# A smaller descriptor space for GpSimd, and two more feature buffers that are loaded early

## The chip, the core and the metric

The kernel runs on one core of a Trainium2 chip. A core has five engines with a queue of instructions each: TensorE (PE in the profile, with PEld for its weight loads), VectorE (DVE), ScalarE (ACT), GpSimd (POOL) and SyncE (SP), and 16 DMA engines that all queues share. The metric is the device time of one execution in microseconds (us). Three runs of the kernel before took 311.9, 312.74 and 313.98 us; the median is 312.74 us.

## What is computed

There are 16384 tokens of 256 features (`r_feat`) and a segment number from 0 to 7 for each (`r_bids`). Here is the reference, cut to what matters:

```python
q, k, v = feat @ Wq, feat @ Wk, feat @ Wv          # 32, 32 and 256 wide
starts = jnp.searchsorted(bids, jnp.arange(B, dtype=bids.dtype))
pos = jnp.arange(N, dtype=bids.dtype) - starts[bids]
# rows are put at [bids, pos] of a (8, 3072) frame; the mask says which places are filled
scores = jnp.einsum('bld,bmd->blm', qp, kp)
attn = softmax(jnp.where(mask[:, None, :], scores, NEG))
rp = jnp.einsum('blm,bmd->bld', attn, vp)
r = rp[bids, pos]
t = r @ Wt
tn = (t - t.mean(axis=0)) / jnp.sqrt(t.var(axis=0) + EPS) * gamma + beta
return feat + relu(tn)
```

The segment numbers are not sorted, so a segment's frame takes in only those of its tokens that lie within 3072 of its start. All other tokens read a row at an edge of a frame. So a few thousand tokens have a row of their own, and every other token gets its features plus one of a few rows that are the same for many tokens. The mean and the variance run over all tokens, so no output can be finished before the attention of all segments is done.

## The kernel before, in words

The program (`fast_path`, from line 900) is written as one list of operations. A small class records which bytes each operation reads and writes, and puts a semaphore wait where two operations on different queues touch the same bytes. Each engine runs its own operations in the order of the list, so the place of a line in the source is its place in its engine's queue.

**Stages.** First come the tables: which tokens belong to which segment, by matrix products and comparisons. Then a loop over the segments `e` = 0 to 7 (lines 1683 to 1830). Segment `e` has 4 to 6 tiles of 128 rows. Its rows are gathered from HBM by GpSimd (`gather`, line 882) into `xs`, two segments ahead; TensorE makes scores and attended rows; they end in `tk`, and SP stores them to `t_rows` in HBM. In the last loop (from line 1895), which I call the tail, the output is written, in two ways:

- *Groups.* The tokens are cut into 16 groups of 1024 tokens, 1 MB of features each. A group is loaded into a buffer `fb[i % NF]` (`group_in`, line 1670, on SP's queue), gets its shared row added, and is stored to `out` as a whole (line 1918). Two groups make a pair, and there are 8 passes `c`, one a pair. In each, TensorE makes the shared rows by a one-hot product (`hot`); VectorE adds half of the buffer, and for the other half TensorE adds the features by an identity product and ScalarE copies the sum back into the buffer. At the end of pass `c` VectorE normalises the own rows of segment `c` (`rows(c)`: two tensor-tensor operations and one more on `tk`).
- *Puts.* The own rows overwrite their places in `out`: GpSimd scatters each tile of 128 rows by an indirect DMA (`put`, line 892). There are 39 puts for the eight segments (their own groups must be stored before), and two for tokens that share a place (`tl`).

**What orders stores, loads and puts.** SP's queue is in order. After store `i` it waits for store `i-2` to land and then counts up the semaphore `done` (`finish`, line 1890); after that come the reloads that are listed for this store:

```python
1670    def group_in(i, after=()):
1671        pg.dma("SP", fb[i % NF][:], feat3[ORDER[i]], after)
1893    LATER = {5: (9, 10), 6: (11, 12), 7: (13,), 8: (14,), 9: (15,)}
1916            f = fb[i % NF]
1920            if i >= 2:
1921                finish(stores[i - 2])
1922                for k_ in LATER.get(i, ()):
1923                    group_in(k_)
```

GpSimd's puts of segment `e` wait until `done` has reached the number of the last group that holds a token of that segment's reach; after that wait the puts follow one another. At the very end GpSimd waits until all puts have landed.

**Memory.** There are 9 group buffers (`NF` = 9, line 956). They lie over the work space of the stages before (from `lm` to `sq`), so they can be loaded only when that part is no longer needed: groups 0 to 4 in the loop over `e` = 6 (lines 1725 to 1769), 5 and 6 in segment 7 (line 1797), 7 and 8 just before the tail (line 1834), and 9 to 15 in the tail by `LATER`. A small buffer `rsq` (line 979) holds squares of the repeated rows; `eb` (two buffers of 2 KB a partition) holds the token codes for the one-hot tables, and `sel`, `st_t` and `ss` lie over it for later use.

GpSimd's indirect DMAs take their descriptors from a space in SBUF that the compiler sets aside, 16 KB of each partition unless another size is given to `bacc.Bacc` (line 1996).

Of the kernel before, what the change touches and what calls it, by code (L numbers as in the profile page):

```python
# [9 lines left out]
F32 = mybir.dt.float32  # L10
# [9 lines left out]
P = 128  # L20
NB = 8
# [6 lines left out]
FT = 6  # L28
# [871 lines left out]
def fast_path(nc, feat, bids, wq, wk, wv, wt, gamma, beta, out, bad):  # L900
    N, D = feat.shape
# [4 lines left out]
    GT = 8  # L906
# [9 lines left out]
    end = start  # L916
    plan = []

    def at(name, shape, dtype, off):
        h = nc.alloc_sbuf_tensor_at(name, shape, dtype, offset=off)  # L920
        pg.place(h, "SB", off, mybir.dt.size(dtype))
        return h

    def new(name, shape, dtype=F32):
        nonlocal end
        size = mybir.dt.size(dtype)
        for d in shape[1:]:
            size *= d
        plan.append((name, shape, dtype, end))
        h = at(name, shape, dtype, end)  # L930
        end += size + -size % 32
        return h

    def addr(h):
        return pg.where[h.name][1]
# [5 lines left out]
    lm = new("lm", [P, NL, J + 3], BF16)  # L941
# [11 lines left out]
    vs[1] = new("vs1", [P, FT, D + 1])  # L953
    pb = new("pb", [P, FT, QB])
    sq = [new(f"sq{i}", [P, D]) for i in range(4)]
    NF = 9
    fb = [at(f"f{i}", [P, GT, D], F32, addr(lm) + 8192 * i) for i in range(NF)]
    assert end >= addr(lm) + 8192 * NF

    ident, ones, irow = new("ident", [P, P]), new("ones", [P, P]), new("irow", [P, P])  # L960
    ones_n = new("ones_n", [P, P])
# [3 lines left out]
    xl, tl = new("xl", [P, LT, D]), new("tl", [P, LT, D])  # L965
    eb = [new("eb0", [P, GT * P], BF16), new("eb1", [P, GT * P], BF16)]
    sel = at("sel", [P, FT, P], F32, addr(eb[0]))
    st_t = at("st_t", [P, 2 * D], F32, addr(eb[0]))
    ss = at("ss", [P, 2 * D], F32, addr(eb[1]))
    ye = at("ye", [P, D], F32, addr(acc) + 1024)  # L970
# [5 lines left out]
    cbeg, cend, n_bc = new("cbeg", [P, NL]), new("cend", [P, NL]), new("n_bc", [P, NL])  # L976
    n_1 = new("n_1", [P, NL])
    later = new("later", [P, 2])
    rsq, cnt7, e7, ew = new("rsq", [P, D]), new("cnt7", [P, 2]), new("e7", [P, 2]), new("ew", [P, 2, FT])
    mask, idx = new("mask", [P, TT]), new("idx", [P, TT + LT], I32)  # L980
    reads_r, rdens = new("reads_r", [P, TT]), new("rdens", [P, TT])
    jc, lr, pad = new("jc", [P, FT]), new("lr", [P, FT]), new("pad", [P, FT])
# [231 lines left out]
    def gather_reads(e, tiles, after):  # L1214
        for t in tiles:
            m = e * FT + t
            pg.gather(reads_r[:, m : m + 1], reads_of, idx[:, m : m + 1], N, after=[after])
# [262 lines left out]
    def slot(n=1):  # L1480
        for _ in range(n):
            if work:
                work.pop(0)()
# [155 lines left out]
    def one_hot():  # L1639
        C = NG // 2  # L1640

        def part(c):
            def go():
                x = eb[c % 2]
                pg.set("DVE", x[:], 99.0)
                for r in range(2):
                    pg.dma(
                        "SP", x[64 * r : 64 * r + 6 * NB, :],
                        edge_of[ORDER[2 * c + r] * GT * P : (ORDER[2 * c + r] + 1) * GT * P].unsqueeze(0).to_broadcast(
                            [6 * NB, GT * P]  # L1650
                        ),
                    )

            def end():
                pg.ts(hot[:, c, :, :], eb[c % 2][:].rearrange("e (p i) -> e i p", i=GT), emod[:], ALU.is_equal)

            return go, end

        ps = [part(c) for c in range(C)]
        todo = [ps[0][0]]  # L1660
        for c in range(C):
            if c + 1 < C:
                todo.append(ps[c + 1][0])
            todo.append(ps[c][1])
        return todo
# [4 lines left out]
    def group_in(i, after=()):  # L1670
        pg.dma("SP", fb[i % NF][:], feat3[ORDER[i]], after)

# [20 lines left out]
    for e in range(NB - 1):  # L1693
        n = e + 1
        for eng in ("PE", "ACT", "DVE"):
            pg.register(eng, n, tiles_i[0:1, n : n + 1], 2)
        if e == 1:
            todo, choose = tables()
            work.extend(todo)
        if e == 2:  # L1700
            work.extend(one_hot())
            work.append(choose)
        ahead = e + 2
        LTs = FT if ahead < NB else LT
        for u in range(FT):
            if ahead <= NB and u == 0 and e:
                first = list_half(ahead, 0, ps_s[2])
            attend(e, u)
            if e == 0 and u == 0:
                second_list()  # L1710
                attended(e, u)
                first = list_half(ahead, 0, ps_s[2])
            if ahead <= NB and u == 0:
                first()
                if LTs == FT:
                    second = list_half(ahead, 1, ps_s[3])
            slot(int(u in steps.get(e, range(FT))))
            if u == 4 and e + 3 <= NB and e:
                list_tests(e + 3, FT if e + 3 < NB else LT)
            if u == 4:  # L1720
                values(n, 0)
            if u == 5:
                values(n, 1)
            if e == NB - 2 and u == 3:
                group_in(1)
            if (e, u) != (0, 0):
                opened = attended(e, u)
            if u == 0:
                if ahead <= NB and LTs == FT:
                    second()  # L1730
                if ahead == NB:
                    others()
                xt_main(n, 0)
                xt_main(n, 1)
            if u == 1:
                xt_rest(n)
                project(n, 0)
                scores(e, 1, None)
            if u == 3:
                project(n, 1)  # L1740
                scores(n, 0, range(4))
            if u == 4:
                scores(n, 0, range(4, 6))
            if u == 5:
                values(n, 2)
            for x in ready:
                moments(*x)
            ready = []
            lag.append((e, u))
            for _ in range(0 if e == 0 else 2 if u % 2 else 1):  # L1750
                if lag:
                    square(*lag[0])
                    ready.append(lag.pop(0))
            if e == 0 and u == 1:
                pg.tr32(gb[:].rearrange("p s i -> p (s i)"), graw[:].rearrange("p s i -> p (s i)"))
                for e_ in range(3, NB):
                    pg.dma(
                        "SP", xs[:, e_ * FT : (e_ + 1) * FT, :], zt[:].unsqueeze(1).to_broadcast([P, FT, D]), [opened]
                    )
            if e == 0 and u in (1, 5):  # L1760
                pg.copy("ACT", spot[:], ones[:, 0:1])
            if (e, u) in reads_at:
                gather_reads(*reads_at[e, u], opened)
            if e == NB - 2 and u == 1:
                group_in(0)
            if e == NB - 2 and u > 3:
                group_in(u - 2)
            if e == NB - 2 and u == 5:
                group_in(4)
            if e == 4 and u == 3:  # L1770
                pg.set("POOL", tk[:, TT - 2 : TT, :], 0.0)
                pg.register("POOL", "writes", writes[:], 16 * (6 * NB + LT), 16 * (4 * NB + LT - 1))
                pg.register("POOL", "lastg", lastg[:], NG, 1)
                pg.register("POOL", "third", third_l[:], 1)
                for e_ in range(NB):
                    pg.register("POOL", ("g", e_), upto[0:1, e_ : e_ + 1], NG, 1)
                    pg.register("POOL", e_, tiles_i[0:1, e_ : e_ + 1], 2)
    slot(99)

    e = NB - 1  # L1780
# [13 lines left out]
    for u in range(4):  # L1794
        attend(e, u)
        if u == 3:
            group_in(5)
            group_in(6)
        if u == 0:
            pg.tt(weights, weights, ew[:, 0, :], ALU.add)  # L1800
        if u == 3:
            attended(e, u)
            choose_rows(0)
            choose_rows(1)
        for x in ready:
            moments(*x)
        ready = [(e, u)]
        if u == 1:
            for t in range(3, FT):
                m = e * FT + t  # L1810
                pg.ts(by_reads[:, t - 3, :], ones_n[:], reads_r[:, m : m + 1], ALU.mult)
        if u != 3:
            attended(e, u)
        if u == 2:
            scores(e, 1, None)
        if u < 3:
            repeated(u)
# [13 lines left out]
    pg.mm(sums[:], we[:], ecat[0 : 2 * NB, :, :].rearrange("p s d -> p (s d)"), start=False, stop=True)  # L1831
    choose_rows(3)
    pg.mm(b_e[:, 0:D], ident[:], ecat[:, 0, :], start=False, stop=True)
    for i in range(7, NF):
        group_in(i)
    for t in range(LT):
        pg.gather(tl[:, t, :], t_rows, ridl[:, t : t + 1], NB * FW)
# [1 line left out]
    def unit(i, x):  # L1839
        return fb[i % NF][:, x : x + 2, :].rearrange("p t d -> p (t d)")  # L1840

# [48 lines left out]
    def finish(w):  # L1890
        pg.op("SP", lambda e: e.sem_inc(done, 1), [], [], after=[w])  # L1891

    LATER = {5: (9, 10), 6: (11, 12), 7: (13,), 8: (14,), 9: (15,)}
    stores = []
    for c in range(NG // 2):
        pair = (2 * c, 2 * c + 1)
# [18 lines left out]
        for i in pair:  # L1915
            f = fb[i % NF]
            stores.append(
                pg.op("SP", lambda e, i=i, f=f: e.dma_start(out3[ORDER[i]], f[:]), [f[:]], [], dma=True)
            )
            if i >= 2:  # L1920
                finish(stores[i - 2])
                for k_ in LATER.get(i, ()):
                    group_in(k_)
# [86 lines left out]
```

## Time and profile before

| | |
|---|---|
| median of three runs | 312.74 us |
| the profiled execution | 313.58 us |
| its span, first to last instruction | 311.3 us |
| busy: PE, DVE, ACT, POOL | 254.0, 226.2, 138.7, 132.9 us |
| moved by DMA | 56.81 MB |
| group loads, group stores | 16 each, of 1024 KB |
| puts of segment rows, of repeated rows | 39 and 2 |
| mean granted TensorE clock | 0.918 |

Times in the profile are microseconds from the start of the span, unless a duration is given in ns (the mean of a group of instructions, or minimum, median and maximum). A row of the timeline has start, length, engine, line, operation, what is written and read, and in brackets how long the engine had been idle and what ended that. The engine's name with a q (SPq, POOLq) means its sequencer. "Landing" is the time from the issue of a DMA to its completion. The line of an instruction is often that of a helper, so the tile's name tells more. In a table of stretches the columns are busy time with the number of instructions for PE, PEld, DVE, ACT and POOL (or for POOL alone), then the granted clock, the busy share of the DMA engines, and GB/s.

### The profile page before, as it was taken

The page shows a single profiled execution, that of the slowest core. Times are in us where ns is not written, and L with a number is a line of the kernel's source. Part 1 is how long each engine was busy: PE and PEld are TensorE (multiplying, and loading weights), DVE is VectorE, ACT ScalarE, POOL GpSimd, SP SyncE. Part 2 cuts the span into 40 slices and gives each one's busy share as a digit, 9 for nine tenths or more (in the row PEclk, how much of TensorE's full clock was granted, in tenths as well). Part 3 has the DMA queues.
Part 4 walks back from the last instruction along what each step waited for, and adds up shares of the span by engine and source line. Part 5 has one row for each costly group of instructions (what it writes and reads, how often), then busy time and mean ns, then how long its engine had stood idle before and what let it go on. Part 6 is the DMA issues. An engine that isn't in the chain of part 4 may idle for free.

```text
span 311.3 us, 4501 instructions
## 1 busy us (share of the span) xinstructions
PE 254.0 (82%) x1204; PEld 168.3 (54%) x1204; DVE 226.2 (73%) x712; ACT 138.7 (45%) x298; POOL 132.9 (43%) x155
## 2 busy tenths in 40 slices
PE   1779688899798898999999999989969978673800
PEld 1655565766576677687868778757533322221200
DVE  7866778679999896737664774777389999992820
ACT  7346234267474728544754583564432222121110
POOL 3435580340250061006322754742230278887774
PEclk9989796999999999999999999999998977789565
DMA  3102069422122021112131321679997899999995
GB/s 98 35 24 60 11 194 346 161 87 69 52 75 78 28 75 30 67 57 80 32 95 36 90 90 28 196 244 379 359 394 312 365 346 420 425 419 418 418 411 193
DMA packets 23238, 56.81 MB, mean 183 GB/s; under 512 B 4768, under 2 KB 15858, under 8 KB 19114
## 3 DMA queue, kind: packets, MB, share of 16 engines
q1 hardware_dynamic: 17434, 45.77, 39.5%
q0 software_dynamic: 5232, 10.18, 10.1%
q10 hardware_dynamic: 544, 0.52, 0.5%
q8 instruction: 13, 0.21, 0.3%
q14 instruction: 15, 0.12, 0.1%
HBM read 26.73 MB, written 28.61 MB: 178 GB/s over the span
## 4 chain that ended last, share of the span: by engine, by line
PE 40%; DVE 31%; DMA 11%; issue 7%; ACT 6%; POOL 2%; SPq 1%; DVEq 0%; POOLq 0%; ACTq 0%
PE ps L807 38%; DMA out<-f 6%; DMA f<-in_r_feat 5%; DVE acc L846 4%; DVE tk L826 2%; DVE w L826 2%; DVE f L826 2%; DVE junk L833 2%; POOL out L892 2%; PE ps L812 2%; DVE k L823 2%; ACT pa L817 1%; DVE ge L835 1%; ACT xT L817 1%; ACT tk L817 1%
## 5 line engine op out<-in xcount | busy, mean ns | idle before, releaser
L882 POOL DMA_INDIRECT xs<-in_r_feat,idx x48 | 51.0, 1063 | 101.5 <-DVE idx L846 77.3
L807 PE MATMUL ps<-vs,pa 128*128 128x257 f32 x312 | 73.6, 384 | 4.7 <-ACT sq L817 3.6
L807 PEld LDWEIGHTS ps<-vs,pa 128*128 128x128 f32 x312 | 57.2, 190 | 16.5 <-ACT sq L817 4.8
L892 POOL DMA_INDIRECT out<-tk,idx x39 | 46.1, 1182 | 25.9 <-SPq L1891 14.6
L807 PE MATMUL ps<-f,ident 128*128 128x512 f32 x64 | 41.8, 778 | 12.8 <-DMA f<-in_r_feat 12.8
L817 ACT ACTIVATE tk<-ps,rdens 128x256 f32<-128x256 f32 x46 | 22.2, 482 | 61.8 <-DVE rdens L859 61.7
L822 ACT COPY f<-ps 128x512 f32<-128x512 f32 x32 | 17.1, 590 | 53.3 <-PE ps L807 53.3
L807 PE MATMUL ps<-wvt,xT 128*128 128x256 f32 x156 | 39.7, 406 | 0.3 <-ACT pa L817 0.3
L807 PEld LDWEIGHTS ps<-wvt,xT 128*128 128x128 f32 x156 | 31.1, 204 | 11.0 <-issue 4.3
L807 PEld LDWEIGHTS ps<-f,ident 128*128 128x128 f32 x64 | 13.3, 235 | 29.1 <-DMA f<-in_r_feat 17.1
L846 DVE SCALAR_TENSOR_TENSOR acc<-sq,reads_r,acc 128x256 f32<-128x256 f32 x45 | 21.6, 480 | 8.8 <-ACT sq L817 8.8
L817 ACT ACTIVATE pa<-ps,mask 128x512 f32<-128x512 f32 x39 | 24.0, 689 | 7.6 <-PE ps L807 7.4
L826 DVE TENSOR_TENSOR f<-f,ps 128x512 f32<-128x512 f32 x32 | 20.0, 682 | 7.7 <-DMA f<-in_r_feat 7.1
L826 DVE TENSOR_TENSOR tk<-tk,ss 128x1024 f32<-128x1024 f32 (+1 forms) x30 | 24.4, 850 | 0.3
L882 POOL DMA_INDIRECT reads_r<-reads_of,idx x12 | 13.4, 1119 | 24.8 <-ACT sq L817 11.9
L846 DVE SCALAR_TENSOR_TENSOR acc<-tk,reads_r,acc 128x256 f32<-128x256 f32 x45 | 21.5, 478 | 1.2 <-ACT tk L817 0.7
L807 PE MATMUL ps<-q,k 32*128 32x512 f32 (+2 forms) x154 | 21.1, 482 | 1.5 <-ACT pa L817 1.1
L807 PE MATMUL ps<-xT,w 128*128 128x512 f32 (+1 forms) x60 | 20.7, 478 | 0.6 <-ACT xT L817 0.5
L823 DVE COPY k<-ps 32x128 f32<-32x128 f32 x40 | 11.8, 294 | 12.2 <-PE ps L807 11.3
L807 PE MATMUL ps<-vs,pb 128*128 128x257 f32 x82 | 19.6, 387 | 0.0
L807 PEld LDWEIGHTS ps<-vs,pb 128*128 128x128 f32 x82 | 15.1, 189 | 6.5 <-issue 2.3
L817 ACT ACTIVATE q<-ps,cqk 96x512 f32<-96x512 f32 (+3 forms) x24 | 14.6, 607 | 7.7 <-PE ps L807 7.4
(258 smaller groups left out, 355.3 us busy)
## 6 DMA issues: line engine op xcount, KB each, us to landing
f<-in_r_feat SPq DMA_DIRECT2D x16, 1024.0 KB, 11.7
out<-f SPq DMA_DIRECT2D x16, 1024.0 KB, 10.3
t_rows<-tk SPq DMA_DIRECT2D x8, 512.0 KB, 4.8
xs<-zt SPq DMA_DIRECT2D x5, 768.0 KB, 10.5
t_rows<-tk SPq DMA_DIRECT2D x8, 256.0 KB, 2.3
eb<-edge_of SPq DMA_DIRECT2D x16, 96.0 KB, 2.3
xs<-in_r_feat,idx POOLq DMA_INDIRECT x48, 2.8
out<-tk,idx POOLq DMA_INDIRECT x39, 7.3
```

The lines of the kernel that those rows point to most:

```text
L807: "PE", lambda e: e.matmul(out, lhsT, rhs, start=start, stop=stop, skip_group_check=True),
L812: return self.op("PE", lambda e: e.transpose(out, in_, ident), [in_, ident], [out])
L817: "ACT", lambda e: e.activation(out, in_, func, bias=bias, scale=scale), [in_, *more], [out]
L822: return self.op("ACT", lambda e: e.copy(out, in_), [in_], [out])
L823: return self.op(eng, lambda e: e.tensor_copy(out, in_), [in_], [out])
L826: return self.op(eng, lambda e: e.tensor_tensor(out, a, b, op), [a, b], [out])
L833: lambda e: e.tensor_scalar(out, a, s1, s2, op0, op1, accum_out=accum)
L835: else e.tensor_scalar(out, a, s1, s2, op0, op1),
L846: else e.scalar_tensor_tensor(out, a, s, b, op0, op1),
L882: lambda e: e.indirect_dma_start(out=out, out_offset=None, in_=table, in_offset=bass.IndirectOffsetOnAxis(ap=ind, axis=0), bounds_check=n ...
L892: lambda e: e.indirect_dma_start(out=table, out_offset=bass.IndirectOffsetOnAxis(ap=ind, axis=0), in_=src, in_offset=None, bounds_check=n ...
```

## The change

The descriptor space becomes 2 KB instead of 16 KB of each partition. In the room, two more group buffers are made that don't lie over the work space, so `NF` becomes 11 and `NE`, the number of buffers apart, is 2. Groups 0 and 1 are loaded into these in the fifth segment (`e` = 4, after its tiles 0 and 3). The loads that stood later keep their places, with group numbers higher by two. In the tail five groups are reloaded instead of seven, each behind an earlier store. `rsq` moves into the second half of `eb[1]`.

```diff
-    NF = 9
-    fb = [at(f"f{i}", [P, GT, D], F32, addr(lm) + 8192 * i) for i in range(NF)]
-    assert end >= addr(lm) + 8192 * NF
+    NF, NE = 11, 2
+    over_work = [at(f"f{i}", [P, GT, D], F32, addr(lm) + 8192 * (i - NE)) for i in range(NE, NF)]
+    assert end >= addr(lm) + 8192 * (NF - NE)
+    fb = [new(f"f{i}", [P, GT, D]) for i in range(NE)] + over_work
...
     sel = at("sel", [P, FT, P], F32, addr(eb[0]))
+    rsq = at("rsq", [P, D], F32, addr(eb[0]) + 3072)
...
-    rsq, cnt7, e7, ew = new("rsq", [P, D]), new("cnt7", [P, 2]), new("e7", [P, 2]), new("ew", [P, 2, FT])
+    cnt7, e7, ew = new("cnt7", [P, 2]), new("e7", [P, 2]), new("ew", [P, 2, FT])
...
             if e == NB - 2 and u == 3:
-                group_in(1)
+                group_in(NE + 1)
...
+            if e == NB - 4 and u in (0, 3):
+                group_in(int(u == 3))
             if e == NB - 2 and u == 1:
-                group_in(0)
+                group_in(NE)
             if e == NB - 2 and u > 3:
-                group_in(u - 2)
+                group_in(NE + u - 2)
             if e == NB - 2 and u == 5:
-                group_in(4)
+                group_in(NE + 4)
...
         if u == 3:
-            group_in(5)
-            group_in(6)
+            group_in(NE + 5)
+            group_in(NE + 6)
...
-    for i in range(7, NF):
+    for i in range(NE + 7, NF):
         group_in(i)
...
-    LATER = {5: (9, 10), 6: (11, 12), 7: (13,), 8: (14,), 9: (15,)}
+    LATER = {4: (11,), 5: (12,), 6: (13,), 7: (14,), 8: (15,)}
...
-    nc = bacc.Bacc("TRN2", target_bir_lowering=False, num_devices=1)
+    nc = bacc.Bacc("TRN2", target_bir_lowering=False, num_devices=1, dynamic_dma_scratch_size=2048)
```

## The prediction, made before the changed kernel ran

> **What bounds the kernel now.** I read the page's slices first, then the stretches of the tail, then the queue of GpSimd (POOL), and last who waits for the feature groups.
>
> ```profile
> span 311.3 us, 4501 instructions
> ...
> DMA  3102069422122021112131321679997899999995
> ...
> PE 40%; DVE 31%; DMA 11%; issue 7%; ACT 6%; POOL 2%; SPq 1%; DVEq 0%; POOLq 0%; ACTq 0%
> ```
> ```profile
> 140.00:190.00 50.00, 50.00 (x285) 39.29 (x284) 32.43 (x100) 29.30 (x70) 23.04 (x21) 1.00 0.24 71
> 231.00:254.00 23.00, 20.07 (x91) 7.11 (x88) 22.73 (x36) 8.49 (x16) 7.15 (x6) 0.92 0.87 334
> 254.00:282.00 28.00, 21.46 (x72) 7.13 (x72) 27.06 (x41) 5.94 (x12) 22.71 (x18) 0.76 1.02 419
> 282.00:300.00 18.00, 7.54 (x18) 2.52 (x18) 9.07 (x11) 2.65 (x6) 14.04 (x14) 0.75 1.01 416
> 300.00:311.30 11.30, 0.00 (x0) 0.00 (x0) 0.00 (x0) 0.00 (x0) 6.17 (x7) 0.50 0.66 258
> ```
>
> The columns of the stretches are PE, PEld, DVE, ACT and POOL, then clock, DMA share and GB/s. From 140 to 190 TensorE is busy in every microsecond and the DMA engines are at a quarter. From 254 to 300 the DMA engines are full at 416 to 419 GB/s, and VectorE is full only to 282. At first sight the tail belongs to the transfers, and the change takes two of them, 2 x 1024 KB, out of it. Then I looked at POOL, which has seven instructions after 300 and is the last to stop.
>
> ```profile
> 252.10 0.98 POOL L892 DMA_INDIRECT out<-tk,idx  x1 [0.30 <-issue]
> 254.11 1.89 POOL L892 DMA_INDIRECT out<-tk,idx  x1 [1.02 <-SPq L1891]
> 256.30 1.63 POOL L892 DMA_INDIRECT out<-tk,idx  x1 [0.30 <-issue]
> ...
> 294.84 0.98 POOL L892 DMA_INDIRECT out<-tk,idx  x1 [0.30 <-issue]
> 296.13 1.55 POOL L892 DMA_INDIRECT out<-tk,idx  x1 [0.31 <-DVE tl L826]
> ...
> 305.72 0.98 POOL L892 DMA_INDIRECT out<-tl,idx  x1 [0.31 <-issue]
> 307.00 0.99 POOL L892 DMA_INDIRECT out<-tl,idx  x1 [0.30 <-issue]
> ```
> ```profile
> L892 POOL DMA_INDIRECT out<-tk,idx x39: 983/984/1892, 247.0 to 304.4; - x39
> ...
>   SPq L1891: 14.6, 2
>   issue: 11.3, 37
> ...
> DMA to landing us min/median/max: 3.4/7.1/9.1
> ```
> ```profile
> 254.00:308.00 54.00, 42.91 (x37) 0.72 1.00 407
> ```
>
> This is the reading that decides for me. From 254.11 to 307.99 POOL issues 37 scatters ("puts") back to back: 42.91 us of work and 36 steps of 0.30, which is 53.7 of 53.9 us. It waits for nothing in all that time. The put at 296.13 that the trace lays on VectorE had 0.31 of idle, the common step, so the page's chain, which there leaves POOL for VectorE and the transfers, has taken a wrong turn. After 254.11 the end is POOL's own queue: 307.99, then the last put's landing, then about 1 us of closing waits.
>
> **What starts that queue.** POOL waits twice (14.6 us at SP's line 1891): before the first put, at 247.02, and at 254.11. From the indices of seed 0 I worked out the groups that each segment's puts must follow: 3, 5, 5, 7, 7, 7, 11, 11 finished stores for segments 0 to 7, whose tiles are 4, 4, 5, 6, 6, 6, 4, 4 (39, the count above). The code reports a finished store only after the issue of the store two further on, so count 3 comes after store 4 and count 5 after store 6.
>
> ```profile
> 245.72 0.84 SPq L1918 DMA_DIRECT2D out<-f  x2
> ...
> 252.83 0.34 SPq L1918 DMA_DIRECT2D out<-f  x1
> ```
>
> 245.72 and 252.83 lie 1.3 us ahead of the two put starts, and those stores wait for the sums of pairs 2 and 3, on a VectorE busy 22.73 of 23 us. Nothing there waits for a load.
>
> **The change, part by part.**
>
> *Two loads leave the tail.* In segment 6 to 7 nine loads are issued before and nine after, with group numbers two higher; nothing moves there. Behind the stores there are five reloads where there were seven, each one or two stores earlier. What this frees is shown by who waits for a group:
>
> ```profile
> PE ps L807 <- DMA f<-in_r_feat: 12.8, 5, 6.1
> ...
> DVE f L826 <- DMA f<-in_r_feat: 7.1, 2, 6.5
> ```
> ```profile
> 289.37 1.88 DVE L826 TENSOR_TENSOR f<-f,ps 128x512 f32<-128x512 f32 x3 [6.53 <-DMA f<-in_r_feat]
> ```
>
> VectorE loses 7.1 us, 6.5 of them before the last pair (289.37). These go: the last sums, the last rows and the repeated rows come about 7 us earlier, and the last stores leave the queue about 2 x 1.05 MB / 419 GB/s = 5.0 us earlier. On the path that sets the end this is worth nothing, since the puts that need those rows already found them ready. Its cover is POOL's queue; without it 5.0 us would be won (a rival below).
>
> *What is left of it on the path.* The last put lands 3.4 us after its start at 307.00, with stores still in flight. With the stores gone about 5 us sooner it meets emptier engines. The gathers, most of them in stretches at a quarter load, show what that is worth:
>
> ```profile
> DMA to landing us min/median/max: 2.1/2.9/7.2
> ```
>
> 3.4 to 2.9 is -0.5 us; the bounds are 0 and 2.1 - 3.4 = -1.3.
>
> *The length of the puts.* They are long where VectorE works on rows beside them:
>
> ```profile
> 254.00:278.00 24.00, 19.63 (x15) 0.78 1.02 419
> 278.00:308.00 30.00, 23.29 (x23) 0.67 0.98 397
> ```
>
> That is 1.31 us each up to 278 and 1.01 after. Until 282 VectorE is full (27.06 of 28), so its work can't move earlier and the first stretch stays. After it, 8 us of VectorE work slide from 290 to 298 down to 282 to 291, under other puts. It lengthened a put there by up to 0.57 us (296.13: 1.55 against 0.98); others take that place. Zero, give or take 0.6.
>
> *Two loads in the fifth segment.* That is where TensorE is busy 50.00 of 50, with the DMA engines at 0.24. Two issues on SP of some 0.4 us, between row stores, pass no wait: the buffers are new and nothing read them. Each 1 MB takes 2.5 us of the engines at 419 GB/s. What follows on the queue are `edge_of` loads, which are issued two work slots ahead of their use, and the gathers for a later segment. I take zero; if both loads held up TensorE in full, +5.0.
>
> *rsq inside eb1.* It is written in segment 7, and the last reader of eb1 is VectorE's one-hot comparison at the end of segment 6; `ss` follows the last reader of rsq on the same engine. Zero, with no new wait on the path.
>
> *The descriptor space of 2 KB.* What it costs to use the space again is not in this trace with certainty, so I bound it. A full space would hold a put back until an older one has landed. The puts land in at most 9.1 us and start 1.29 apart at the closest, so about 7 are under way at once; the gathers, at most 7.2 us, are fewer. By the Trainium skill (DMA: Bandwidth & Descriptors, "SWDGE vs HWDGE vs iDMA" and "The descriptor swizzle") each engine's descriptors are 16 B, kept in a ring in SBUF, 9 each way for 128 partitions; 2048 / 16 / 9 = 14 puts is then an estimate of what fits, and 7 in flight agrees with no stall.
>
> What remains is a cost for each put, to see that an old place is free. A put costs 0.984 at its fastest, and the gathers when the space was fresh the same:
>
> ```profile
> 14.09 1.00 POOL L882 DMA_INDIRECT xs<-in_r_feat,idx  x1 [0.30 <-issue]
> ```
> ```profile
> L882 POOLq MOVE  x73: 29/29/35, 10.3 to 230.2; - x73
> ```
>
> So nothing in a put's time grows with what lies in the space, and a smaller space can't save anything: the lower bound is 0. The upper bound is one more step such as the 0.30 between puts, 37 x 0.30 = +11.1 us. With 73 gathers (one move each) and 41 puts, the last put, at 307.00, is the 114th indirect transfer; it took 0.99 like the rest; I lean on that and take 0.
>
> **Sum.** 0 (loads) - 0.5 (landing) + 0 (puts) + 0 (segment 4) + 0 (rsq) + 0 (space) = -0.5. The profiled execution took 313.58 us, its span 311.3 and 2.3 around it; it becomes 313.1. It is 0.8 above the median of the runs shown, 312.74, so I say 312.2.
>
> **The rivals.**
>
> *The transfers set the end.* For it: DMA share 1.02 and 419 GB/s in the tail, the page's chain, and 12.8 us of TensorE's waits. Against it: 37 puts without one wait. If the puts are paced by the transfers after all, 5.0 us go: 307.7. The Trainium skill (DMA: Bandwidth & Descriptors, "Issuing engines are not separate DMA queues") speaks for this rival: all queues share 16 engines, so less work there means an earlier end. The row against it is the put pitch, 1.29 under full engines and in the last 5 us alike.
>
> *Using the space again costs time at every put.* This is the slower side. Place: POOL, from the moment the small space has gone round once, which is long before 254. Price p on each of the 37 puts, with no cover, because that queue is the end. From p = 0.10 us it makes the kernel slower by over 1% (37 x 0.10 - 0.5 = +3.2); at p = 0.30 it gives 312.7 + 11.1 - 0.5 = 323.3, at 0.13 about 317. For it: the queue has no slack and before had nearly a fresh place for every transfer. Against it: the even 0.98.
>
> *The early loads hold up TensorE in segment 4.* It has no idle time to give there. Against it: DMA share 0.24. +5.0 - 0.5 gives 317.2.
>
> *The change doesn't do what it says*, so that the last pair still waits, perhaps since the reloads bunch up behind stores 4 to 8. Then nothing moves, 312.7; in time this can't be told from my forecast.
>
> **How the numbers follow.** Forecast, with the last rival's time inside it, 0.66; transfers set the end 0.10; costly reuse of the space 0.19, of which over half above 1%, and half of it within the range; segment 4 slowed 0.05. The forecast's own range is 311.0 to 314.0. To leave out no more than 0.2 I take in the first rival (307.7) below, and above the reuse up to 0.13 us a put: 307.5 to 317.0. A measurement of this kernel tells about 1% (3.1 us) from no change; faster by over that holds 0.11, within it 0.67, slower 0.22.
>
> **What would show it.** Right: the puts after the second wait run with 0.30 between them and 0.98 at the fastest, from about 254 to 308; the wait of VectorE for the last pair's group is gone; the last store is issued some 5 to 8 us before 299.8; and the end has not moved. Wrong on the transfers: puts shorter, or POOL finishing several microseconds before 308. Wrong on the space: a fastest put or a step longer than 0.984 and 0.30, or idle time before puts laid on older puts. Wrong on segment 4: TensorE waiting for a transfer between 140 and 190, and everything after shifted. The forecast as a whole falls if the first two put starts move from 247.0 and 254.1, since all its terms lie behind them.

## The result, and the profile after

The kernel became slower: 321.59 us against 313.36 us (medians of six runs of each, alternated on one chip), a ratio of 1.0268 with a 95% interval of 1.0232 to 1.0304. I had said 312.2 and no change. Here and below medians are over all runs, and ratios over the fast runs alone, without those more than 1.5% above the fastest of the same kernel (in experiment 6 one run of 1322.52 us). The profiled execution took 321.46 us, 2.4 of them outside its span of 319.1.

First the page's slices and the first line of its chain, as I read them for the kernel before:

```profile
span 319.1 us, 4502 instructions
...
DMA  3102089221211120224513123799979999999422
...
POOL 2%; issue 1%; POOLq 0%
```

The DMA engines were full up to the last slice; now the last three hold 4, 2 and 2 tenths. So the transfers end earlier and the kernel ends later. The chain is POOL alone, and it breaks off after 3% of the span: the trace names nothing that released POOL.

The stretches, with the columns as before:

```profile
140.00:190.00 50.00, 50.00 (x285) 39.28 (x284) 31.47 (x93) 29.90 (x70) 22.54 (x22) 1.00 0.35 111
231.00:254.00 23.00, 20.31 (x81) 7.40 (x82) 22.72 (x35) 7.63 (x15) 8.71 (x8) 0.89 0.87 322
254.00:282.00 28.00, 23.18 (x84) 7.55 (x82) 27.52 (x43) 7.52 (x14) 16.90 (x14) 0.91 1.02 422
282.00:300.00 18.00, 0.99 (x7) 0.41 (x6) 7.21 (x9) 1.07 (x2) 11.85 (x11) 0.62 0.91 369
300.00:319.10 19.10, 0.00 (x0) 0.00 (x0) 0.00 (x0) 0.00 (x0) 12.84 (x13) 0.50 0.23 78
```

In the fifth segment TensorE is still busy in 50.00 of 50, with the DMA share up from 0.24 to 0.35: the two early loads cost nothing there. From 254 to 282 POOL (the fifth pair of numbers) fell from 22.71 us with 18 puts to 16.90 with 14, while nothing else got slower. After 300 POOL works alone.

The timeline of POOL tells why. These are the last put before the second wait, the first after it, the puts around the two places where the spacing changes, and the last one:

```profile
251.06 0.98 POOL L892 DMA_INDIRECT out<-tk,idx  x1 [0.30 <-issue]
253.15 1.80 POOL L892 DMA_INDIRECT out<-tk,idx  x1 [1.11 <-SPq L1895]
...
268.61 1.12 POOL L892 DMA_INDIRECT out<-tk,idx  x1 [0.30 <-issue]
277.18 1.49 POOL L892 DMA_INDIRECT out<-tk,idx  x1 [7.44 <-issue]
278.97 0.99 POOL L892 DMA_INDIRECT out<-tk,idx  x1 [0.30 <-issue]
...
295.91 0.98 POOL L892 DMA_INDIRECT out<-tk,idx  x1 [0.30 <-issue]
300.83 0.98 POOL L892 DMA_INDIRECT out<-tk,idx  x1 [3.93 <-issue]
...
316.32 1.00 POOL L892 DMA_INDIRECT out<-tl,idx  x1 [0.30 <-issue]
```

Two steps are not 0.30 us but 7.44 and 3.93. Counted from the first put, they stand before the 15th and before the 29th, 14 puts apart. The trace has 48 packets for a put. When the first stretch began, 483 packets of puts had landed; when it ended, 672, which is 14 x 48 exactly. At the end of the second it was 1344, 28 x 48. Each time POOL went on only when no put was under way any more.

The groups of puts, then POOL's waits, from the kernel before and from the kernel after:

```profile
L892 POOL DMA_INDIRECT out<-tk,idx x39: 985/987/1867, 246.1 to 313.7; - x39
...
DMA to landing us min/median/max: 2.3/6.4/8.8
```
```profile
POOL out L892 <- issue: 11.3, 37, 0.3
```
```profile
POOL out L892 <- issue: 22.0, 37, 7.4
```

The puts themselves are as short as before (985 ns at the fastest, against 983). "Issue", the idle time to which the trace gives no cause, grew from 11.3 to 22.0 us over the same 37 steps, and its longest went from 0.3 to 7.4.

With the rows above, the span's 7.9 us add up. The second start came 0.96 earlier (254.11 to 253.15). The two stretches cost 7.44 + 3.93 - 2 x 0.30 = 10.77. The 37 puts took 42.44 us, 0.47 less:

```profile
253.00:318.00 65.00, 42.44 (x37) 0.71 0.77 313
```

From the last put's end (316.32 + 1.00) to the end of the span it was 1.8 us where it had been 3.3, so -1.43; all of it is the last put's landing, 2.3 us where it had been 3.8. -0.96 + 10.77 - 0.47 - 1.43 = 7.91.

What the change was to do otherwise, it did: VectorE's wait of 7.1 us for a feature group is gone, and what is left of TensorE's is

```profile
PE ps L807 <- DMA f<-in_r_feat: 0.8, 1, 0.8
```

The last group store was issued at 290.3; before it was at 299.8:

```profile
L1922 SPq DMA_DIRECT2D out<-f x16: 332/332/882, 231.9 to 290.3; - x16
```
```profile
299.79 0.33 SPq L1918 DMA_DIRECT2D out<-f  x1
```

### The profile page after: what moved, and what is told of

It is laid out like the page before. It is cut to its first block, busy times and chain, and to the rows that moved or that the text cites. A ratio compares the mean times of both kernels' runs of the same rounds, so it can differ in the third digit from the quotient of the medians.

```text
span 319.1 us, 4502 instructions
## 1 busy us (share of the span) xinstructions
PE 248.1 (78%) x1204; PEld 165.9 (52%) x1204; DVE 226.8 (71%) x712; ACT 139.0 (44%) x298; POOL 132.3 (41%) x155
## 5 line engine op out<-in xcount | busy, mean ns | idle before, releaser
L807 PE MATMUL ps<-f,ident 128*128 128x512 f32 x64 | 36.1, 692 | 0.8 <-DMA f<-in_r_feat 0.8
L882 POOL DMA_INDIRECT reads_r<-reads_of,idx x12 | 14.1, 1176 | 25.8 <-ACT sq L817 12.1
L807 PE MATMUL ps<-y,hot 48*128 48x256 bf16 x128 | 14.9, 281 | 9.0 <-DVE f L826 6.9
L807 PE MATMUL ps<-xT,w 128*128 128x512 f32 (+1 forms) x60 | 19.3, 452 | 0.6 <-ACT xT L817 0.5
L807 PEld LDWEIGHTS ps<-f,ident 128*128 128x128 f32 x64 | 12.2, 210 | 14.2 <-issue 11.8
L807 PEld LDWEIGHTS ps<-y,hot 48*128 48x128 bf16 x128 | 5.2, 94 | 27.3 <-issue 12.3
```

The lines of the kernel that those rows point to most:

```text
L807: "PE", lambda e: e.matmul(out, lhsT, rhs, start=start, stop=stop, skip_group_check=True),
L882: lambda e: e.indirect_dma_start(out=out, out_offset=None, in_=table, in_offset=bass.IndirectOffsetOnAxis(ap=ind, axis=0), bounds_check=n ...
```

## The experiments

These theories were open. **A**: a place of the small space is free again only when all puts issued so far on its semaphore have landed; the puts share one, so a full space makes POOL wait for everything under way. **B**: the moved loads and the closer stores hold the puts up, and the space has no part in it. **C**: my rival, a price at every put for using the space again. **D**: a full space is emptied as a whole, however the semaphores are dealt out. Beside them stood **P**, that POOL's queue of puts is the end, and **T**, that the transfers set it.

The first put starts somewhere between 243 and 251 us in the profiled executions. Partly that comes from a pause of TensorE near 185 us, of 0.6 to 2.5 us in seven of the profiles and absent in the others. It does not go with an edit: the changed kernel has it in its second profile (1.46 us) and not in its first. So I compare executions from the second start of the puts on, and take times only from runs that alternated with the kernel before on the same chip. Where a line was added above, line 892 is 893.

**1 and 2. The small space alone.** The kernel before, with nothing changed but the size, 2 KB and then 4 KB:

```diff
-    nc = bacc.Bacc("TRN2", target_bir_lowering=False, num_devices=1)
+    nc = bacc.Bacc("TRN2", target_bir_lowering=False, num_devices=1, dynamic_dma_scratch_size=2048)
```

> The kernel before with the descriptor space of 2 KB and nothing else (9 buffers, old places of the loads). Theory A, places of puts come free together: a put that meets a full space waits until every put issued so far on the shared semaphore has landed. Then there are two idle stretches of POOL, before the 15th and the 29th put, 4 to 8 us each, as in the changed kernel; about 8 us slower than before, 320 to 322. Rival B, the moved and bunched loads hold up the puts: no idle stretch here and 313.4 us, as before. Rival C of the prediction, a price on each put: the step between puts grows from 0.30 or their least length from 0.984; both would already show in the changed kernel and don't, so no such growth is expected.

> The kernel before with 4 KB. Theory A: 28 places, so a single idle stretch, before the 29th put, until the 28th has landed (about 7 us while stores are in flight); 5 to 7 us slower than before, 318 to 320. Rival B: none, 313.4. If the idle stretches came from something else at these points of the kernel, the one before the 15th put would stay.

With 2 KB: 327.81 us, ratio 1.0364 (1.0273 to 1.0455). That is some 6 us above the expected 320 to 322. In the profile 4.3 us lie ahead of the puts: their second start came at 258.38, against 254.11 in the kernel before. The place was as expected: the only long steps of POOL are before the 15th and the 29th put:

```profile
281.64 0.98 POOL L892 DMA_INDIRECT out<-tk,idx  x1 [6.70 <-issue]
...
307.39 0.98 POOL L892 DMA_INDIRECT out<-tk,idx  x1 [6.58 <-issue]
```

With 4 KB: 320.5 us, 1.0172 (1.0098 to 1.0245), 5.6 us above the kernel before as A had expected (5 to 7), and one long step, before the 29th:

```profile
299.11 1.33 POOL L892 DMA_INDIRECT out<-tk,idx  x1 [7.19 <-issue]
```

B falls: no load was moved here, and the steps are there. C falls as well: the fastest put is 982 and 983 ns, and a price at each put would not come every 14 or 28. The space fills in proportion to its size: 14 puts in 2 KB, 28 in 4 KB. The Trainium skill (DMA: Bandwidth & Descriptors, "Terms", "SWDGE vs HWDGE vs iDMA" and "The descriptor swizzle"), from which I had estimated 14 puts for 2 KB, agrees with these runs in the count.

**3. The changed kernel with a semaphore for every put**, and a wait for each at the end, the 17 puts that are issued under a condition last:

```diff
-                i.then_inc(loose, 16)
+                i.then_inc(o.own, 16)
...
+        o.own = self.nc.alloc_semaphore(f"put_{len(self.puts)}")
...
+    for o in sorted(pg.puts, key=lambda o: o.when is not None):
+        with ExitStack() if o.when is None else pg.given(*o.when):
+            pg.op("POOL", lambda x, s=o.own: x.wait_ge(s, 16), [], [])
...
-    nc.gpsimd.wait_ge(pg.loose, pg.regs[("POOL", "writes")])
```

> The changed kernel (2 KB, two more buffers), but each put counts up a semaphore of its own instead of the one that all puts share; at the end POOL waits for each of them. Theory A: the oldest put's place is known to be free by itself, so there is no idle stretch although the space is as small; 312 to 313.5. A rival D, the space is emptied whole whenever it is full, whatever the semaphores: the same two idle stretches, about 321.5. Rival B: 321.5 too.

322.97 us, 1.0281 (1.0224 to 1.0338): the time missed what A expected by some 10 us. The place did not: no step is longer than 0.31 us, still with 2 KB, and the 37 puts are through in 54.7 us where the changed kernel took 64.2.

```profile
310.01 0.99 POOL L893 DMA_INDIRECT out<-tl,idx  x1 [0.31 <-issue]
```

Its own waits ate the gain: 311.0 is the last put's end and 319.8 the span's. POOL's sequencer was at the conditional waits from 312.4 to 318.2, 5.8 us for 17 branches. I had not counted these. D falls in any case: the space is as small, and nothing is emptied.

**4. The buffers without the small space.** The changed kernel with one extra buffer instead of two, loaded once in the fifth segment, and 10 KB for the descriptors:

```diff
-    NF, NE = 11, 2
+    NF, NE = 10, 1
...
-    LATER = {4: (11,), 5: (12,), 6: (13,), 7: (14,), 8: (15,)}
+    LATER = {4: (10,), 5: (11, 12), 6: (13,), 7: (14,), 8: (15,)}
...
-    nc = bacc.Bacc("TRN2", target_bir_lowering=False, num_devices=1, dynamic_dma_scratch_size=2048)
+    nc = bacc.Bacc("TRN2", target_bir_lowering=False, num_devices=1, dynamic_dma_scratch_size=10240)
```

> One more buffer instead of two, loaded in the fifth segment, with a space of 10 KB (71 places, more than the 41 puts). Theory A: no idle stretch of POOL, so this shows what the buffers alone are worth: 312.5 to 313.5, the end set by the puts as before. If the transfers set the end instead, half of 5.0 us comes off: 310.9. Rival B: slower than before, by some 4 us.

314.21 us, 0.9971 (0.9935 to 1.0007), with no long step. One load fewer in the tail is worth no time that can be told. T's 310.9 stood for 2.5 us off, which beside the 314.88 that the kernel before took on this chip is a ratio of 0.992, just outside the interval. That speaks for P, but by a small margin; experiment 6 is the stronger evidence. The 314.21 itself is above the 312.5 to 313.5 that P had expected, as the kernel before was slower on this chip too.

**5. The third experiment with its conditional waits ahead of the others**, so that they run while the last puts are still landing (the sort's condition is turned round).

> The changed kernel (2 KB, two more buffers) with a semaphore for each put, and at the end the waits for the puts that may not run, with their 17 branches, ahead of the others, so that they fall beside the last puts. Theory A: no idle stretch between puts and no long row of branches behind them: 0.995 to 1.000 of before, some 8 us faster than the changed kernel. Rival D, the space is emptied whole when it is full: two idle stretches, 1.027.

315.58 us, 1.0073 (1.004 to 1.0107). No long step; 1.9% faster than the changed kernel by the two ratios. It missed the expected range on the slow side, and the trace shows 2.6 us from the last packet of a put to the end of the span, where the kernel before has 0.9, and 37 puts that take 44.36 us against 42.91. The second start and the last put were

```profile
253.96 1.80 POOL L893 DMA_INDIRECT out<-tk,idx  x1 [1.11 <-SPq L1899]
...
308.31 0.99 POOL L893 DMA_INDIRECT out<-tl,idx  x1 [0.31 <-DMA out<-tk,idx]
```

**6 to 8. Starting the puts earlier.** By my prediction the queue's start depended on when SP counts up a finished store. Here SP does that for stores 2 and 4 before it issues stores 4 and 6, in the kernel of experiment 5 (6), the kernel before (7) and the one of experiment 4 (8):

```diff
             f = fb[i % NF]
+            if i in (4, 6):
+                finish(stores[i - 2])
...
             if i >= 2:
-                finish(stores[i - 2])
+                if i not in (4, 6):
+                    finish(stores[i - 2])
```

> The same, and SP reports the third and the fifth finished store before it issues stores 4 and 6 instead of after. Theory P, POOL's queue of puts is the end: its first part starts about 2.0 us and the rest about 2.8 us earlier (the fifth store has landed at 249.6, the report came at 253.2), and the end comes as much earlier: 0.987 to 0.991 of before. Theory T, the transfers set the end: no gain over the kernel without this edit.

> The kernel before (16 KB, 9 buffers) with the early report alone. Theory P: puts start 2.0 and 2.8 us earlier, but the puts of segments 6 and 7 must follow the eleventh store, which was reported at 292.9 when POOL came to it at 294.8; so POOL now waits there some 1 to 2 us, and the end comes about 1 us earlier: 0.995 to 0.999. Theory T: 1.000.

> One more buffer, a space of 10 KB, the shared semaphore, and the early report. Theory P: no idle stretch, the eleventh store lands early enough, 2.8 us faster than the same kernel without the early report: 0.986 to 0.991 of before. Theory T: 0.997.

Experiment 6: 312.71 us, 0.9984 (0.9954 to 1.0014). Against the kernel before that misses the expected 0.987 to 0.991, since experiment 5, on which it is built, had missed too. Against experiment 5 on the same chip it is 0.9% less, 2.9 us where P had expected 2.8 and T nothing, and the intervals don't meet. The puts go through without the second wait, about 3 us ahead of experiment 5, where this one started at 253.96:

```profile
250.88 0.98 POOL L893 DMA_INDIRECT out<-tk,idx  x1 [0.31 <-issue]
...
304.74 0.99 POOL L893 DMA_INDIRECT out<-tl,idx  x1 [0.30 <-DMA out<-tk,idx]
```

The last put starts 3.57 us earlier than in experiment 5, 304.74 against 308.31. So a shift of the queue's start is a shift of the end: P, shown by moving it.

Experiment 7: 313.73, 1.0015 (0.9986 to 1.0043), a miss. In the profiled execution the puts start 4 to 5 us earlier and then catch up with the stores that they must follow:

```profile
243.06 1.02 POOL L892 DMA_INDIRECT out<-tk,idx  x1 [9.54 <-DVE f L826]
...
263.87 1.10 POOL L892 DMA_INDIRECT out<-tk,idx  x1 [1.70 <-SPq L1891]
...
292.74 0.98 POOL L892 DMA_INDIRECT out<-tk,idx  x1 [3.48 <-SPq L1891]
```

Without the earlier stores of the new buffers, POOL's queue is no longer the only bound. 1.70 + 3.48 less the steps is 4.6 us. This profiled execution took 311.13 us and was the fastest of the twelve, so it shows the new waits and not the typical time.

Experiment 8: 313.67, 1.0002 (0.9972 to 1.0032), a miss too. In its profiled execution the second part of the puts waited for a store that was issued late, while an identity product of TensorE took 3.68 us (granted clock 0.55 from 240.40 to 244.20) that takes 1.98 four microseconds on (clock 1.00):

```profile
240.44 3.68 PE L807 MATMUL ps<-f,ident 128*128 128x512 f32 x4
...
244.38 1.98 PE L807 MATMUL ps<-f,ident 128*128 128x512 f32 x4
```

Whether that accounts for all of its runs stays open. By their times alone, experiments 7 and 8 are what T had expected (1.000 and 0.997); it is experiment 6, and POOL's new waits in the two traces, that speak for P.

**9 and 10. The changed kernel and the small space alone again**, on one chip:

> The changed kernel once more, on the same chip as the next three. Two idle stretches, before the 15th and the 29th put; 1.025 to 1.030 of before.

> The kernel before with 2 KB alone once more. Theory A with what the first look showed (idle stretches of 6.7 and 6.6 us against 7.4 and 3.9 in the changed kernel): 1 to 3 us slower than the changed kernel, since with two reloads less the stores are out of the way sooner when a put must wait for landings; 1.030 to 1.037. If the buffers are worth nothing here either: the same as the changed kernel.

324.73 us (1.0232; 1.0177 to 1.0287) and 325.56 us (1.0278; 1.0227 to 1.0329), both a little under the expected ranges. The long steps are where they were, in the changed kernel

```profile
279.33 1.93 POOL L892 DMA_INDIRECT out<-tk,idx  x1 [7.00 <-issue]
...
303.15 0.98 POOL L892 DMA_INDIRECT out<-tk,idx  x1 [3.67 <-issue]
```

and with the small space alone

```profile
276.66 0.99 POOL L892 DMA_INDIRECT out<-tk,idx  x1 [6.92 <-issue]
...
300.90 0.98 POOL L892 DMA_INDIRECT out<-tk,idx  x1 [5.79 <-issue]
```

The second step is 2 to 3 us shorter with the buffers (3.93 and 3.67 against 6.58 and 5.79). That fits the stores that end sooner, so that the puts under way land on emptier engines. In time the two can't be told apart (0.5%, inside the intervals), so what the buffers give back stays inconclusive.

**11. The changed kernel with nine semaphores**, one for the puts of each segment and one for the repeated rows; nine waits end the program, on counts that are worked out per segment. The space stays at 2 KB.

```diff
+        self.of = [nc.alloc_semaphore(f"of_seg_{i}") for i in range(NB + 1)]
...
-                i.then_inc(loose, 16)
+                i.then_inc(o.own, 16)
...
+        o.own = self.of[of]
...
+    for e in range(NB + 1):
+        pg.op("POOL", lambda x, e=e: x.wait_ge(pg.of[e], pg.regs[("POOL", ("w", e))]), [], [])
...
-    nc.gpsimd.wait_ge(pg.loose, pg.regs[("POOL", "writes")])
```

> The changed kernel (2 KB, two more buffers), with one semaphore for the puts of each segment and one for the repeated rows, nine in all instead of one; at the end nine waits without branches. Theory A, in the form that a reused place waits for every put issued so far on its own semaphore: when the 15th put comes, all puts of segment 0 have been issued and landed, and so on, hence no idle stretch, though semaphores are still shared: 0.996 to 1.003 of before. A rival, any shared semaphore makes it wait for all puts in the space: two idle stretches, 1.027.

314.98 us, 0.9929 (0.9901 to 0.9957), a little better than the expected 0.996 to 1.003; the changed kernel on the same chip took 324.73. Only the two waits for stores are left, of which the trace names a releaser for the second alone:

```profile
248.49 1.10 POOL L893 DMA_INDIRECT out<-tk,idx  x1 [13.49 <-issue]
...
255.27 1.80 POOL L893 DMA_INDIRECT out<-tk,idx  x1 [1.11 <-SPq L1900]
...
309.61 0.99 POOL L893 DMA_INDIRECT out<-tl,idx  x1 [0.30 <-issue]
```

Semaphores shared by 4 to 6 puts do no harm. When the 15th put needs a place, the puts of the first two segments, which hold the oldest places, have landed, and no later put belongs to their semaphores. A stands. Beside the kernel before, this version gains 0.7% on this chip where experiment 5 lost 0.7% on another, though their puts run alike (37 in 55.3 us in both); from the last packet of a put to the end of the span they differ by only 0.65 us. The rest of that difference I can't explain, so the step from the changed kernel is what I rest on, and not the sign against the kernel before.

**12. The same with the early report of experiment 6.**

> The same with the early report of stores 3 and 5. Theory P, POOL's queue is the end: 2 to 3 us faster than without the early report, 0.989 to 0.996 of before. If the transfers set the end: no gain over it.

313.42 us, 0.988 (0.9823 to 0.9938), the best ratio of all, and faster than both kernels. In the profiles the last put ends at 307.95 instead of 310.60; in time the gain over experiment 11 is 1.6 us, under the expected 2 to 3, and the two intervals overlap:

```profile
245.63 1.02 POOL L893 DMA_INDIRECT out<-tk,idx  x1 [9.20 <-DVE f L827]
...
252.76 0.98 POOL L893 DMA_INDIRECT out<-tk,idx  x1 [1.65 <-SPq L1900]
...
306.96 1.00 POOL L893 DMA_INDIRECT out<-tl,idx  x1 [0.30 <-DMA out<-tk,idx]
```

## Why the prediction was wrong

**The step that failed** is the one on the descriptor space: "A full space would hold a put back until an older one has landed." I took 0 for it. It measured +10.77 us in the trace, and alone it explains the sign. The count before it held: 14 places (the steps stand every 14 puts), and no more under way than the 7 that I had said (when the 15th was due, 483 of 672 packets had landed, so 10 puts' worth, and 4 were out). By that count the 15th put should have found free places. What the runs showed instead is a place that could be used again only when everything issued on its semaphore had landed. With one semaphore for all puts that is the put just issued. POOL then stands still for its landing, 8.6 us from 268.61 to 277.18 where 9.1 had been the longest landing before. This happens twice, 37 + 4 puts being more than 28. Giving up the one semaphore for all puts (experiments 3, 5 and 11) took the steps away at the same size of space; giving the old kernel the small space (experiments 1 and 10) brought them.

**The slower rival** had the sign, the place and the lack of cover right, and the price wrong: not p at each put, but a whole landing at every 14th. My bound of +11.1 held the 10.77, by luck, since it was built from 37 steps of 0.30. My reason for leaning to 0, the even length of the puts, says nothing on this: a wait before a put is not in its length. Nor could the 114th transfer show it: at 14 for 2 KB the 16 KB hold an estimated 112, so only the last two puts took used places, and these had last held the first gathers, which had landed long before.

**POOL's queue is the end**: right. In the changed kernel the transfers ended earlier and the kernel later; experiment 6 moved the queue's start by about 3 us, and the end went with it, in the trace and in time (experiment 12 did so clearly only in the trace). The first rival, that the transfers set the end, fell, and with it my reading of the Trainium skill (DMA: Bandwidth & Descriptors, "Issuing engines are not separate DMA queues") on which I had let it lean. The same section of the Trainium skill says that the time to initiate a DMA is usually small beside the DMA itself. The traces agree for one put (0.98 us at the shortest, against a median landing of 6.4 us in the changed kernel), but 37 of them follow one another on one engine and fill 55.3 us in experiment 11 without a stall, and that queue ends last.

**The loads.** The early ones cost nothing, as I had said (50.00 of 50). The last store came 9.5 us earlier, where I had said 5 to 8; off the path, this cost the forecast nothing.

**Landing:** -1.43, beyond my bound of -1.3, where I had said -0.5. Part of that was a reading: the 3.4 us that I took for the last put is the landing of the put before it, and the last one's is 3.8. It fell to 2.3.

**Length of the puts:** I said 0, give or take 0.6. In the changed kernel it was -0.47, but with stalls. In the versions without them it was 43.74 with one extra buffer (+0.8) and 44.35 with two (+1.4). The stores and VectorE's work closed up beside the puts, and I had assumed that other puts take each other's place. Which of the two lengthens them was not tried.

**The first starts** moved by a microsecond, not more (247.0 to 246.1 and 254.1 to 253.2), so the condition on which I had hung the whole forecast held to within that microsecond, and did not save it.

## What to carry to other kernels

A space for descriptors is not sized by the transfers under way alone: ask also what tells it that a place is free. If many transfers count up one semaphore, each time round the small space can cost a full landing, and on the queue that sets the end nothing covers it. A few semaphores dealt out in the order of issue remove the wait without more space. Before freeing the transfers of a stage, look for the engine whose steps are even to the end, and move its start.

## What the runs showed of the hardware

- A full descriptor space shows in the trace as "issue", with no releaser, of 3.7 to 7.4 us before an indirect DMA of POOL; at 10 and 16 KB no such step appears in 41 puts, at 4 KB one, at 2 KB two. POOL goes on when all puts issued on the shared semaphore have landed (672 and 1344 packets, 48 for each put).
- The 73 gathers go through the same space first, and yet the steps are counted from the first put. The mechanism above accounts for that, though no run tried it apart: the first 14 puts take places that gathers held last, and all gathers had landed (in the changed kernel the last was issued at 233.2, 12.9 us before the first put, and the longest landing of one was 8.2). The gathers themselves count up 48 semaphores in turn, and none of them came while the one 14 before it was still under way; their longest step without a releaser is 0.58 us in the changed kernel, against 0.47 in the kernel before.
- The conditional waits on POOL's sequencer (a branch, and the wait where the put had run) took about 0.34 us each (17 in 5.8 us) at the end of experiment 3.
